# Graph attention in two layers: x projections in pieces of one row tile, with x in another buffer and the edge weights begun earlier

## The chip, the cores and the metric

The kernel runs on one core of a Trainium2 chip. The metric is the device time of one execution in microseconds, and a version of the kernel is judged by the median of its runs. All data is float32 apart from the integer adjacency matrix and a bfloat16 mask.

The core's engines appear under the names that the profile uses: PE is TensorE (its weight loads are shown apart, as PEld), DVE is VectorE, ACT is ScalarE, POOL is GpSimd, and SP is SyncE, which here issues every DMA. Each engine works through its own queue in order and waits on semaphores for the others.

## What is computed

There are 8 entries (the batch), each with 2048 nodes of 256 features. One adjacency matrix of 2048 x 2048 is shared by all. Two layers of graph attention follow one another, each with a residual and a layer norm:

```python
# layer 0: 8 heads of 32 features, prior = adj
x_proj = einsum('bnd,hdf->bhnf', x, W)
e = leaky_relu(e_src[..., :, None] + e_dst[..., None, :], 0.2)
e = e + softplus(beta_tilde) * log(prior + 1e-6)
attn = softmax(where(adj > 0, e, neg_inf), axis=-1)
x = layernorm(x + (attn @ x_proj, heads side by side) @ W_out.T)
# layer 1: one head, 256 features
h1, h2, h3 = x @ W1, x @ W2, x @ W3
attention = softmax(where(adj > 0, leaky_relu(h1 @ h2.T, 0.2), -1e12))
x = layernorm(x + relu(attention @ h3))
```

## The kernel before

**Layer 0 without a matrix of exponentials.** The exponential of a leaky ReLU of a sum is the larger of two products of a row factor and a column factor. So for each head the kernel keeps one vector over the query nodes (`c`, broadcast to all partitions) and a few numbers for each key node (`re`). For a key tile `jt` of 128 nodes (16 tiles: `NT`) and two heads (`HP`), line 311 makes `s = max(c, re) * mt` on VectorE, 128 x 2048 for each head. `mt` is the transposed tile of edge weights, `(adj + 1e-6)**beta` where there is an edge and 0 elsewhere. Then `products` (line 336) multiplies `s` with the projected features `v` into `val`, and with the key factor into `den`: 16 and 16 matmuls with 512 columns. One such unit of work, a pair of heads and a key tile, is a *step*. An entry takes 4 x 16 = 64 steps. `s` has four buffers, which is two steps' worth.

**What comes before the steps of an entry.** `Gat.project` loads x of the entry, transposes it on TensorE (`turn`, lines 235 to 243, one call for four row tiles of 128 nodes, with ScalarE copying to `xt`), multiplies with the projection weights `wp` (line 253, four matmuls for a row tile) and lets ScalarE copy the result to `v` and `both` (lines 255 and 256). When all 16 row tiles are there, a maximum over the nodes is taken (lines 260 and 261), the factors are made (`cs`, `re`), and VectorE scales all of `v` by the key factor (line 270). For entries 1 to 7 the results go to DRAM (`v_d`, `re_d`). At last `est` is a transpose of `cs` and goes to DRAM as `c_d` (lines 277 to 280). `project` is a generator: each `yield` ends a *piece*. There are six pieces for an entry: one for each group of four row tiles, one with the maximum and the scaling of `v`, one with `est`.

**Where those pieces stand.** Entry 0 is projected alone at the start. While entry 0's 64 steps run, the loop at lines 480 to 485 puts the pieces of entries 1 to 7 between them: `(B - 1) * (NB + 2)` = 42 pieces spread evenly over 64 steps. In the same loop `later_weights` prepares the weights that are needed later, in five parts, from step 16 on at every fourth step. Its three square matrices are loaded one after another into the buffer with the tag `pen` and transposed.

**Edge weights.** They are made in entry 0 during its first 16 steps and written to DRAM (`mt_d`), from where all later steps load them (`load_mt`, line 183). `make_mt(jt)` loads a column block of `adj` (tag `d`, two buffers), converts it (VectorE, line 168), takes a logarithm and an exponential (ScalarE, lines 169 and 170), masks it (VectorE, line 171), transposes the sixteen blocks on TensorE (line 176, result `mtp`), copies them to `mt` with ScalarE (line 177) and stores that. `m` has the tag `p` with two buffers; `x` of the entries being projected (`xr`, 1 MB for half an entry) has the same tag and shares these two buffers. In step `jt`, `make_mt` runs for tile `jt + 1`, before the step's own `s` and products.

**What sets the order.** TensorE's instructions run exactly in the order in which the program writes them. For the other engines, and for SyncE's DMA issues, the framework picks an order when the kernel is compiled, by priority and by when things would be ready. A buffer is handed to its next tile when the last reader of the old tile is done.

**What follows.** From entry 1 on, a step of layer 0 for the next entry is woven into layer 1 of the current one (`Dot`). `Dot.scores` uses the tag `pen` for the mask of a row tile, one buffer, and `p` for the scores.

Of the kernel before, what the change touches and what calls it, by code (L numbers as in the profile page):

```python
# [9 lines left out]
F32 = mybir.dt.float32  # L10
# [8 lines left out]
P = 128  # L19
# [8 lines left out]
def kernel(  # L28
# [26 lines left out]
    nc = tc.nc  # L55
    B, N, D = x.shape
    H, _, DH = w_proj.shape
    NT = N // P
    KC = D // P
    BK = 512  # L60
    NB = N // BK
# [3 lines left out]
    IG = BK // P  # L65
# [6 lines left out]
    wide = ctx.enter_context(tc.tile_pool(name="wide", bufs=2))  # L72
# [5 lines left out]
    def mm_tile(name):  # L78
        return ps.tile([P, BK], F32, tag="mm", name=name)

    def wide_tile(name, tag, bufs, dtype=F32):
        return wide.tile([P, N], dtype, tag=tag, name=name, bufs=bufs)
# [6 lines left out]
    ident = const.tile([P, P], F32)  # L89
# [14 lines left out]
    nc.vector.scalar_tensor_tensor(beta[:, 3:4], beta[:, 0:1], 0.0, beta[:, 2:3], ALU.max, ALU.add)  # L104
    beta_c = beta[:, 3:4]

    def load_x(b, half):
        xr = wide.tile([P, NT // 2, D], F32, tag="p", name="xr", bufs=2)
        nc.sync.dma_start(xr, x[b].rearrange("(t p) d -> p t d", p=P)[:, ts(half, NT // 2), :])
        return xr  # L110

    first_x = [load_x(0, half) for half in range(2)]


    wp = const.tile([P, KC, D + 2 * H], F32)
# [17 lines left out]
    def later_weights():  # L133

        nc.sync.dma_start(w3s, w3.rearrange("(k p) d -> p k d", p=P))
        w1t, w2t = (chunk.tile([P, KC, D], F32, tag="pt", name=name, bufs=2) for name in ("w1t", "w2t"))
        for w, dst in ((w_out, wot), (w1, w1t), (w2, w2t)):
            src = wide.tile([P, KC, D], F32, tag="pen", name="square", bufs=1)
            nc.sync.dma_start(src, w.rearrange("(k p) c -> p k c", p=P))
            yield  # L140
            for kc in range(KC):
                t = mm_tile("sq_t")
                for o in range(KC):
                    nc.tensor.transpose(t[:, ts(o, P)], src[:, o, ts(kc, P)], ident)
                nc.scalar.copy(dst[:, kc, :], t[:, 0:D])
        yield
        for dc in range(KC):
            t = mm_tile("w12p")
            for kc in range(KC):
                nc.tensor.matmul(t[:, 0:D], w1t[:, kc, ts(dc, P)], w2t[:, kc, :], start=(kc == 0), stop=(kc == KC - 1))  # L150
            nc.scalar.copy(w12[:, dc, :], t[:, 0:D])
        yield
# [7 lines left out]
    rec_d = dram.tile([B, NP, 4, HALF], F32, name="rec_d")  # L160
    x1_d = dram.tile([B, N, D], F32, name="x1_d")

    def make_mt(jt):

        a = wide.tile([P, NT, P], I32, tag="d", name="adj_t", bufs=2)
        nc.sync.dma_start(a, adj[:, ts(jt, P)].rearrange("(t p) j -> p t j", p=P))
        m = wide.tile([P, NT, P], F32, tag="p", name="m", bufs=2)
        nc.vector.tensor_scalar(m, a, 0.0, None, ALU.max)
        nc.scalar.activation(m, m, AF.Ln, bias=eps_prior)
        nc.scalar.activation(m, m, AF.Exp, scale=beta_c)  # L170
        nc.vector.scalar_tensor_tensor(m, a, 0.0, m, ALU.is_gt, ALU.mult)
        mt = wide_tile("mt", "mt", 2)
        for g in range(NB):
            t = mm_tile("mtp")
            for k in range(IG):
                nc.tensor.transpose(t[:, ts(k, P)], m[:, g * IG + k, :], ident)
            nc.scalar.copy(mt[:, ts(g, BK)], t)
        nc.sync.dma_start(mt_d[ts(jt, P), :], mt)
        return mt

    def load_mt(jt, deep):
        mt = wide_tile("mt", "d" if deep and jt % 2 else "mt", 2)
        nc.sync.dma_start(mt, mt_d[ts(jt, P), :])
        return mt
# [27 lines left out]
    def row_tile(name, bufs=4):  # L212
        return small.tile([P, D], F32, tag="row", name=name, bufs=bufs)


    class Gat:


        def __init__(self, b):
            self.b = b  # L220
            self.units = ((hp, jt) for hp in range(NP) for jt in range(NT))
            self.hts = []
            self.mts = []

        def project(self):


            b = self.b
            kept = "v" if b == 0 else ("h3", "x1t")[b % 2]
            self.v = v = whole.tile([P, NT, D], F32, tag=kept, name="v")  # L230
            both = small.tile([P, NT, 2 * H], F32, name="both", bufs=1)
            xrs, xts = [], []

            def turn(g):
                if g % 2 == 0:
                    xrs.append(load_x(b, g // 2) if b > 0 else first_x[g // 2])
                xt = chunk.tile([P, KC, BK], F32, tag="ht", name="xt", bufs=3)
                for kc in range(KC):
                    t = mm_tile("tr")
                    for k in range(IG):  # L240
                        nc.tensor.transpose(t[:, ts(k, P)], xrs[-1][:, g % 2 * IG + k, ts(kc, P)], ident)
                    nc.scalar.copy(xt[:, kc, :], t)
                xts.append(xt)

            turn(0)
            for g in range(NB):
                if g + 1 < NB:
                    turn(g + 1)
                for k in range(IG):
                    it = g * IG + k  # L250
                    t = mm_tile("proj")
                    for kc in range(KC):
                        nc.tensor.matmul(t[:, 0:D + 2 * H], xts[g][:, kc, ts(k, P)], wp[:, kc, :],
                                         start=(kc == 0), stop=(kc == KC - 1))
                    nc.scalar.copy(v[:, it, :], t[:, 0:D])
                    nc.scalar.copy(both[:, it, :], t[:, D:D + 2 * H])
                yield
            top = small.tile([P, 2, H], F32, name="top", bufs=1)
            ed, es = both[:, :, 0:H], both[:, :, H:2 * H]
            nc.vector.tensor_reduce(top[:, 0, :], ed.rearrange("p t h -> p h t"), AX.X, ALU.max)  # L260
            nc.gpsimd.partition_all_reduce(top[:, 1, :], top[:, 0, :], P, bass_isa.ReduceOp.max)
            cs = small.tile([P, H, NT], F32, name="cs", bufs=1)
            nc.vector.tensor_tensor(cs, es.rearrange("p t h -> p h t"),
                                    top[:, 1, :].unsqueeze(2).to_broadcast([P, H, NT]), ALU.add)
            nc.vector.tensor_tensor(ed, ed, top[:, 1:2, :].to_broadcast([P, NT, H]), ALU.subtract)
            self.re = re = small.tile([P, 2, NT, H], F32, name="re", bufs=2)
            nc.scalar.activation(re[:, 0], ed, AF.Exp, scale=-(1.0 - ALPHA))
            nc.scalar.activation(re[:, 1], ed, AF.Exp)
            v4 = v.rearrange("p t (h f) -> p (t h) f", f=DH)
            nc.vector.tensor_tensor(v4, v4, re[:, 1].rearrange("p t h -> p (t h)").unsqueeze(2).to_broadcast(  # L270
                [P, NT * H, DH]), ALU.mult)
            if b > 0:
                nc.sync.dma_start(v_d[b], v)
                nc.sync.dma_start(re_d[b], re)
            yield
            t = mm_tile("est")
            nc.tensor.transpose(t[:, 0:P], cs.rearrange("p h t -> p (h t)"), ident)
            est = row_tile("est")[:, 0:P]
            nc.scalar.activation(est, t[:, 0:P], AF.Exp, scale=1.0 - ALPHA)
            nc.sync.dma_start(c_d[b].rearrange("h (t p) -> (h t) p", p=P), est)  # L280
            yield
# [13 lines left out]
        def step(self, count=1):  # L295

            for _ in range(count):
                hp, jt = next(self.units)
# [3 lines left out]
                    self.den = pacc.tile([P, HALF], F32, tag="den", name="den")  # L302
                first = self.b == 0 and hp == 0
                while first and len(self.mts) < min(jt + 2, NT):
                    self.mts.append(make_mt(len(self.mts)))
                mt = self.mts[jt] if first else load_mt(jt, self.b == 0)
                s = []
                for a in range(HP):
# [4 lines left out]
                v, e = self.v, self.re[:, 1]  # L313
# [161 lines left out]
    for _ in gats[0].project():  # L475
        pass
    others = (1 for g in gats[1:] for _ in g.project())
    weights = later_weights()
    pieces = (B - 1) * (NB + 2)
    for k in range(NP * NT):  # L480
        gats[0].step()
        for _ in range((k + 1) * pieces // (NP * NT) - k * pieces // (NP * NT)):
            next(others)
        if k >= NT and k % 4 == 0:
            next(weights, None)
    for _ in others:
        pass
# [57 lines left out]
```

## Time and profile before

| | us |
|---|---|
| runs, median (lowest to highest) | 4468.5 (4466.72 to 4468.73) |
| the profiled execution | 4467.18 |
| its span in the profile | 4465.4 |
| VectorE, `s` (line 311), 1024 instructions | 2350.6 |
| TensorE, `val` (line 336), 8192 matmuls | 1045.3 |
| TensorE, `den` (line 336), 5568 matmuls | 709.2 |
| TensorE, `acc` (line 461), 4096 matmuls | 950.6 |
| last `den` of entry 0's steps ends, from the start of the span | 538.7 |

The times of instructions are busy times. Matmuls are pipelined, and the records of neighbouring ones overlap, so a busy share of TensorE near 100% means that it had work, and not that it ran at its peak. A timeline row gives a start, a time, the engine, the line, the operation with its output and inputs, how many instructions are merged in it, and in brackets how long the engine was idle just before and who released it. Rows of one engine that follow without a bracket have no gap between them. A busy share is a mean over stages with different limits, so the stretches of the span have to be looked at one by one.

### The profile page before, as it was taken

The numbers are of one execution on the slowest core, as the hardware profiler recorded it, in microseconds if no ns is written. First come the engines' busy times: TensorE is split into PE (matmuls) and PEld (weight loads), VectorE is DVE, ScalarE is ACT, GpSimd is POOL, SyncE is SP. The second block draws the span as 40 slices with busy tenths as digits, with TensorE's granted clock in tenths as the row PEclk, the third lists the DMA queues.
The fourth block names the chain that finished last, engine by engine and source line by source line (L and its number), as shares of the span: only waits on it lengthen the run. The fifth ranks groups of instructions, "written<-read, shape, count | busy, mean of one in ns | idle before, by whom it ended". The sixth has DMA issues, their size and how long they took to land.

```text
span 4465.4 us, 60558 instructions
## 1 busy us (share of the span) xinstructions
PE 4267.6 (96%) x24988; PEld 2217.3 (50%) x24988; DVE 3631.8 (81%) x2605; ACT 1758.7 (39%) x3611; POOL 7.5 (0%) x14
## 2 busy tenths in 40 slices
PE   6899899999999999999999999999999999999899
PEld 4444344445455545555455544545454554554566
DVE  5778798888989988988899888888988888898222
ACT  5622233334333343334333343333433343333555
POOL 0000000000000000000000000000000000000000
PEclk8999999999999999999999999999999999999999
DMA  7777665666555555556555565555545565553211
GB/s 217 262 264 263 249 218 204 220 233 217 180 189 193 182 193 184 188 181 224 176 182 178 186 213 187 189 181 207 194 160 190 189 216 183 187 182 134 69 50 41
DMA packets 252773, 843.62 MB, mean 189 GB/s; under 512 B 33616, under 2 KB 152400, under 8 KB 176976
## 3 DMA queue, kind: packets, MB, share of 16 engines
q1 hardware_dynamic: 252496, 839.74, 54.0%
q8 instruction: 196, 3.21, 0.3%
q14 instruction: 81, 0.66, 0.0%
HBM read 763.76 MB, written 75.37 MB: 188 GB/s over the span
## 4 chain that ended last, share of the span: by engine, by line
PE 60%; DVE 14%; issue 8%; ACT 4%; DMA 1%; SPq 0%; DVEq 0%; ACTq 0%
PE acc L461 17%; PE e L426 15%; PE val L336 12%; DVE s L311 9%; PE den L336 8%; PE pt L445 4%; DVE d L318 3%; PE h1p L416 2%; ACT p L432 1%; PE h3p L396 1%; ACT h L210 1%; DVE p L431 1%; PE y L376 1%; DMA mt<-mt_d 0%; ACT f L206 0%
## 5 line engine op out<-in xcount | busy, mean ns | idle before, releaser
L311 DVE SCALAR_TENSOR_TENSOR s<-c,re,mt 128x2048 f32<-128x2048 f32 x1024 | 2350.6, 2343 | 209.6 <-PE den L336 159.9
L336 PE MATMUL val<-s,v 128*32 128x512 f32 x8192 | 1045.3, 607 | 78.7 <-DVE s L311 78.5
L461 PE MATMUL acc<-h,pts 128*128 128x256 f32 x4096 | 950.6, 380 | 14.9 <-ACT pts L447 14.4
L426 PE MATMUL e<-x1t,h 128*128 128x512 f32 x2048 | 904.0, 594 | 0.0
L461 PEld LDWEIGHTS acc<-h,pts 128*128 128x128 f32 x4096 | 748.2, 190 | 107.7 <-ACT pts L447 21.8
L336 PE MATMUL den<-s,re 128*32 128x512 f32 x5568 | 709.2, 598 | 0.0
L318 DVE SCALAR_TENSOR_TENSOR d<-s,re,d 128x2048 f32<-128x2048 f32 x272 | 632.4, 2343 | 0.0
L426 PEld LDWEIGHTS e<-x1t,h 128*128 128x128 f32 x2048 | 379.6, 190 | 450.1 <-issue 417.9
L336 PEld LDWEIGHTS val<-s,v 128*32 128x32 f32 x8192 | 240.9, 110 | 697.8 <-issue 526.3
L447 ACT COPY pts<-pt 128x512 f32<-128x512 f32 x512 | 296.1, 583 | 664.7 <-PE pt L445 664.4
L428 ACT ACTIVATE p<-e 128x512 f32<-128x512 f32 x512 | 302.5, 595 | 432.3 <-PE e L426 432.3
L431 DVE CUSTOM_DVE_ANT_0 p<-p,pen 128x2048 f32<-128x2048 f32 x128 | 292.7, 2287 | 205.9 <-ACT p L428 205.6
L336 PEld LDWEIGHTS den<-s,re 128*32 128x32 f32 x5568 | 194.2, 112 | 426.7 <-issue 426.6
L432 ACT ACTIVATE p<-p,neg 128x2048 f32<-128x2048 f32 x128 | 256.7, 2005 | 272.5 <-DVE neg L431 272.5
L445 PEld LDWEIGHTS pt<-ident,p 128*128 128x128 f32 x2048 | 238.0, 141 | 223.5 <-issue 167.2
L445 PE MATMUL pt<-ident,p 128*128 128x128 f32 x2048 | 318.7, 279 | 5.4 <-ACT p L432 5.4
L469 DVE TENSOR_TENSOR z<-z,x1r 128x256 f32<-128x256 f32 x128 | 54.0, 422 | 205.4 <-ACT z L468 197.0
L468 ACT ACTIVATE z<-acc,rec 128x256 f32<-128x256 f32 x128 | 60.6, 473 | 355.9 <-PE acc L461 330.3
L376 PE MATMUL y<-wot,ht 128*128 128x256 f32 x512 | 129.6, 414 | 37.4 <-DVE ht L363 36.3
L206 ACT ACTIVATE f<-mv,eps_ln 128x1 f32<-128x1 f32 x256 | 74.2, 290 | 199.0 <-DVE mv L204 198.1
L396 PE MATMUL h3p<-w3s,x1t 128*128 128x256 f32 x512 | 133.4, 386 | 12.3 <-ACT x1t L392 12.3
L376 PEld LDWEIGHTS y<-wot,ht 128*128 128x128 f32 x512 | 104.7, 208 | 68.3 <-DVE ht L363 39.2
(76 smaller groups left out, 2083.6 us busy)
## 6 DMA issues: line engine op xcount, KB each, us to landing
mt<-mt_d SPq DMA_DIRECT2D x496, 1024.0 KB, 4.8
c<-c_d SPq DMA_DIRECT2D x64, 1024.0 KB, 6.7
pen<-pen_d SPq DMA_DIRECT2D x112, 512.0 KB, 3.3
xr<-in_x_dram SPq DMA_DIRECT2D x16, 1024.0 KB, 7.1
adj_t<-in_adj_dram SPq DMA_DIRECT2D x16, 1024.0 KB, 6.8
mt_d<-mt SPq DMA_DIRECT2D x16, 1024.0 KB, 5.6
rb<-rec_d SPq DMA_DIRECT2D x64, 256.0 KB, 4.0
h<-in_x_dram SPq DMA_DIRECT2D x32, 512.0 KB, 5.9
```

The costliest lines, as they stand in the source:

```text
L311: nc.vector.scalar_tensor_tensor(sa, self.cs[a], self.re[:, 0, jt, h:h + 1], mt, ALU.max, ALU.mult)
L318: nc.vector.scalar_tensor_tensor(d, sa, e[:, jt - 1, h:h + 1], d, ALU.mult, ALU.add)
L336: nc.tensor.matmul(dst[ts(q, DH), ts(c, BK)], weights[q % 2], s[q % 2][:, ds(q // 2 * HALF + c * BK, BK)], start=start, stop=stop)
L376: nc.tensor.matmul(y[:, 0:D], ht[:, ts(it, P)], wot[:, g, :], start=(g == 0), stop=(g == 1))
L396: nc.tensor.matmul(t[:, 0:D], x1t[:, kc, ts(it - 1, P)], w3s[:, kc, :], start=(kc == 0), stop=(kc == KC - 1))
L426: nc.tensor.matmul(t, self.h1[:, kc, ts(it % IG, P)], self.x1t[:, kc, ts(c, BK)], start=(kc == 0), stop=(kc == KC - 1))
L428: nc.scalar.activation(p[:, ts(c, BK)], t, AF.Prelu, alpha=ALPHA)
L431: nc.vector.tensor_tensor_reduce(p, p, pen, -1.0, FMAX, ALU.add, ALU.min, neg)
L432: nc.scalar.activation(p, p, AF.Exp, bias=neg, scale=-1.0, accum_out=den)
L445: nc.tensor.transpose(t[:, ts(k, P)], p[:, ts(g * IG + k, P)], ident)
L447: nc.scalar.copy(pt, t)
L461: nc.tensor.matmul(acc, now[:, ts(k, P)], self.h3[:, j, :], start=(j == 0), stop=(j == NT - 1))
```

## The change

Four things are edited.

1. `project` yields after each row tile instead of after each group of four, so it has `NT + 2` = 18 pieces for an entry instead of six, and the loop spreads 7 x 18 = 126 pieces over the 64 steps. The next group's `turn` is called after the first row tile of a group, where it used to be called ahead of the whole group.
2. For entries 1 to 7, `turn` loads the x of its own four row tiles (512 KB) into a tile with the tag `pen`, which has one buffer. Entry 0's x is loaded as before, into the tag `p`.
3. `make_mt` is split. `make_m` does the part up to line 171, and `make_mt` the transposes. In step `jt` of the first 16, `make_m` runs for tile `jt + 2` and then `make_mt` for tile `jt + 1`.
4. `later_weights` loads each square matrix as two row tiles (tag `row`, four buffers) with two DMAs, and its parts come at steps 18, 22, 26, 30 and 34 instead of 16, 20, 24, 28 and 32.

```diff
-    def load_x(b, half):
-        xr = wide.tile([P, NT // 2, D], F32, tag="p", name="xr", bufs=2)
-        nc.sync.dma_start(xr, x[b].rearrange("(t p) d -> p t d", p=P)[:, ts(half, NT // 2), :])
-        return xr
-
-    first_x = [load_x(0, half) for half in range(2)]
+    first_x = [wide.tile([P, NT // 2, D], F32, tag="p", name="xr", bufs=2) for _ in range(2)]
+    for half, xr in enumerate(first_x):
+        nc.sync.dma_start(xr, x[0].rearrange("(t p) d -> p t d", p=P)[:, ts(half, NT // 2), :])
...
-            src = wide.tile([P, KC, D], F32, tag="pen", name="square", bufs=1)
-            nc.sync.dma_start(src, w.rearrange("(k p) c -> p k c", p=P))
+            src = [row_tile("square") for _ in range(KC)]
+            for o in range(KC):
+                nc.sync.dma_start(src[o], w[ts(o, P), :])
...
-    def make_mt(jt):
+    def make_m(jt):
...
         nc.vector.scalar_tensor_tensor(m, a, 0.0, m, ALU.is_gt, ALU.mult)
+        return m
+
+    def make_mt(jt, m):
+
         mt = wide_tile("mt", "mt", 2)
...
             def turn(g):
-                if g % 2 == 0:
-                    xrs.append(load_x(b, g // 2) if b > 0 else first_x[g // 2])
+                if b == 0:
+                    xr = first_x[g // 2][:, ds(g % 2 * IG, IG), :]
+                else:
+                    xr = wide.tile([P, IG, D], F32, tag="pen", name="xg", bufs=1)
+                    nc.sync.dma_start(xr, x[b].rearrange("(t p) d -> p t d", p=P)[:, ts(g, IG), :])
...
             turn(0)
-            for g in range(NB):
-                if g + 1 < NB:
+            for it in range(NT):
+                g, k = divmod(it, IG)
+                t = mm_tile("proj")
+                for kc in range(KC):
+                    nc.tensor.matmul(t[:, 0:D + 2 * H], xts[g][:, kc, ts(k, P)], wp[:, kc, :],
+                                     start=(kc == 0), stop=(kc == KC - 1))
+                nc.scalar.copy(v[:, it, :], t[:, 0:D])
+                nc.scalar.copy(both[:, it, :], t[:, D:D + 2 * H])
+                if k == 0 and g + 1 < NB:
                     turn(g + 1)
-                for k in range(IG):
...
                 yield
...
                 while first and len(self.mts) < min(jt + 2, NT):
-                    self.mts.append(make_mt(len(self.mts)))
+                    at = len(self.mts)
+                    while len(self.ms) < min(at + 2, NT):
+                        self.ms.append(make_m(len(self.ms)))
+                    self.mts.append(make_mt(at, self.ms[at]))
...
-    pieces = (B - 1) * (NB + 2)
+    pieces = (B - 1) * (NT + 2)
...
-        if k >= NT and k % 4 == 0:
+        if k >= NT and k % 4 == 2:
             next(weights, None)
```

More of the change, by code (lines that the diff above doesn't have):

```diff
@@ L143, in later_weights @@
                 for o in range(KC):
-                    nc.tensor.transpose(t[:, ts(o, P)], src[:, o, ts(kc, P)], ident)
+                    nc.tensor.transpose(t[:, ts(o, P)], src[o][:, ts(kc, P)], ident)
                 nc.scalar.copy(dst[:, kc, :], t[:, 0:D])
@@ L222, in __init__ @@
             self.hts = []
-            self.mts = []
+            self.ms, self.mts = [], []
         def project(self):
@@ L231, in project @@
             both = small.tile([P, NT, 2 * H], F32, name="both", bufs=1)
-            xrs, xts = [], []
+            xts = []
             def turn(g):
-                if g % 2 == 0:
-                    xrs.append(load_x(b, g // 2) if b > 0 else first_x[g // 2])
+                if b == 0:
[3 more added lines that the diff above has]
+                    nc.sync.dma_start(xr, x[b].rearrange("(t p) d -> p t d", p=P)[:, ts(g, IG), :])
                 xt = chunk.tile([P, KC, BK], F32, tag="ht", name="xt", bufs=3)
@@ L240, in turn @@
                     for k in range(IG):
-                        nc.tensor.transpose(t[:, ts(k, P)], xrs[-1][:, g % 2 * IG + k, ts(kc, P)], ident)
+                        nc.tensor.transpose(t[:, ts(k, P)], xr[:, k, ts(kc, P)], ident)
                     nc.scalar.copy(xt[:, kc, :], t)
@@ L245, in project @@
             turn(0)
-            for g in range(NB):
-                if g + 1 < NB:
-                    turn(g + 1)
-                for k in range(IG):
[L250 to L256, printed above, removed]
+            for it in range(NT):
[7 more added lines that the diff above has]
+                if k == 0 and g + 1 < NB:
+                    turn(g + 1)
                 yield
```

## The prediction

> **What bounds the kernel now.** I read the busy shares of the page first, then its forty slices, then the busy times by stretch, then the engines' timelines over entry 0's part, and last SyncE's waits.
>
> ```profile
> PE 4267.6 (96%) x24988; PEld 2217.3 (50%) x24988; DVE 3631.8 (81%) x2605; ACT 1758.7 (39%) x3611; POOL 7.5 (0%) x14
> PE   6899899999999999999999999999999999999899
> DVE  5778798888989988988899888888988888898222
> ```
>
> A slice is 111.6 us. TensorE is below 9 in the first three slices, in the sixth and in one near the end. The change touches only what ends at about 545 us, so only there can time come or go. By stretch (span, then PE, PEld, DVE, ACT, POOL, clock, DMA share, GB/s):
>
> ```profile
> 65.30:203.80 138.50, 115.05 (x824) 68.50 (x823) 108.31 (x56) 99.48 (x156) 0.36 (x1) 0.95 0.76 245
> 410.00:470.00 60.00, 55.68 (x399) 24.68 (x391) 47.43 (x24) 15.06 (x46) 0.36 (x1) 0.97 0.72 267
> ```
>
> In the first stretch, where `m` is made, no engine is full: steps 1 to 14 go from the `val` at 67.26 to that at 203.76, 10.5 us each. VectorE waits in nearly every one, for a buffer of `m` or for `mt`:
>
> ```profile
> 188.21 2.28 DVE L171 SCALAR_TENSOR_TENSOR m<-adj_t,m 128x2048 f32<-128x2048 int32 x1
> 193.21 1.23 DVE L168 TENSOR_SCALAR m<-adj_t 128x2048 f32<-128x2048 int32 x1 [2.71 <-PE mtp L176]
> 194.35 4.61 DVE L311 SCALAR_TENSOR_TENSOR s<-c,re,mt 128x2048 f32<-128x2048 f32 x2
> 204.62 4.62 DVE L311 SCALAR_TENSOR_TENSOR s<-c,re,mt 128x2048 f32<-128x2048 f32 x2 [3.46 <-ACT mt L177]
> ```
>
> In the second stretch TensorE is the bound, with one hole per entry, where VectorE scales all of `v` (L270) while two steps follow one another with no projections between them:
>
> ```profile
> 466.44 4.43 DVE L270 TENSOR_TENSOR v<-v,re 128x4096 f32<-128x4096 f32 x1 [0.64 <-ACT re L268]
> ...
> 413.92 1.04 PE L336 MATMUL val<-s,v 128*32 128x512 f32 x2 [2.57 <-DVE s L311]
> 416.18 2.78 PE L336 MATMUL val<-s,v 128*32 128x512 f32 x11 [1.22 <-DVE s L311]
> 417.91 1.06 PE L336 MATMUL den<-s,re 128*32 128x512 f32 x1
> 418.74 1.02 PE L336 MATMUL val<-s,v 128*32 128x512 f32 x3
> 418.76 2.72 PE L336 MATMUL den<-s,re 128*32 128x512 f32 x15
> 421.42 0.33 PE L277 MATMUL est<-ident,cs 128*128 128x128 f32 x1
> ```
>
> The first is VectorE's row of the next hole, the rest TensorE's of this one; the hole returns at 473.19, 59.3 us later. The step takes 421.42 - 413.92 = 7.50 us, against 1.74 + 1.72 = 3.46 for the undisturbed one at 421.67 to 425.13. With the idle 2.57 before it that is 6.6 us lost for each entry; of the 4.0 inside the step 1.22 is idle and 2.8 is slow clock.
>
> Two rows show what a load of x will meet:
>
> ```profile
> L372 SPq DMA_DIRECT2D h<-in_x_dram x4: 384/427/497, 483.3 to 496.4; - x4
> DMA to landing us min/median/max: 6.0/6.5/8.3
> SPq L183 <- DVE s L311: 120.7, 29, 7.9
> ```
>
> The `h` load is the same shape as the new one: four row tiles of x, 512 KB. The last line is SyncE's wait between 200 and 540 us: 120.7 us in all it stood at an `mt` load waiting for `s`, 29 times, 4.2 us on average.
>
> **What the Trainium skill says.** "TensorE: Matmul & The Clock Gate", Part 1 (the HAM clock gate): after an idle window of about 3.4 us the clock falls to half, until about 3.4 us of work. The trace agrees: the step above runs at half speed after 2.57 + 1.22 us idle. "DMA: Bandwidth & Descriptors", Anatomy of one DMA: a DMA's semaphore wait is held by the issuing sequencer, not by the DMA engines; the 120.7 us agree, and what is queued behind waits too. "Trainium Kernel Development and Optimization", Best Practices, asks for double buffers to overlap DMA with compute; the new x buffer is single, which no row of before shows.
>
> **The change part by part.**
>
> *Pieces.* 42 pieces become 7 x 18 = 126, so a step gets two instead of two in three. Piece n falls in step (n+1)/2 at first, later in (n+2)/2; entries start in steps 0, 9, 18, 27, 37, 46, 55. TensorE's work is unchanged: 32 matmuls for a step 3.46 us, a row tile 3.8/4 = 0.95, a turn of 8 transposes 0.93. Each change between `den`, projections and `val` costs about 0.1 (`den` 1.83 instead of 1.72 when transposes follow; 16 projections 3.86 instead of 3.76 when `val` follows). About 22 more steps hold filler, two changes each, 4.4 us; a fifth of it lies in VectorE's shadow: +3.5.
>
> *x in the mask's single buffer.* `turn(0)` and `turn(1)` both stand in an entry's first piece. The load for `turn(1)` can't be issued until the 8 transposes of `turn(0)` release the buffer, and TensorE takes its orders as written: all later `val` and `den` wait behind these transposes, and VectorE after them, since four `s` buffers are two steps. Load 6.5 us from issue (the `h` row). SyncE stands at an `mt` load 120.7/340 = 36% of the time, for about 2.1 more us when met halfway, so with its other queueing (`v_d`, L273, and the rest) I take 1.2. Cover: the two copies of `xt` (0.59 us each, the last ends some 0.75 after the transposes) are followed by the first row tile's 0.95 and nothing else. Of the time from release only the row tile is work, and with the gap between turn and row tile counted as lost: 6.5 + 1.2 - 0.95 + 0.45 for the wake-up and issue = 7.2 idle. Slow clock after it: 2.8, as in the step above. So 10.0 per entry. Bounds: 6.0 landing with a free SyncE and one slow window, 7; 8.3 landing behind `v_d`'s 2 MB (itself 6.5 us to landing), 18. The other two turns have four pieces, two steps, about 12 us, for the same 7.7: nothing. The next entry's first load has five steps.
>
> *What that hides.* In the new order an entry's `v` scaling (piece 16) stands one step before this wait. While TensorE waits for x, VectorE does its 6 us (`top`, `cs`, `both`, 4.43) and the next two `s`. So the 6.6 us hole should go: it is replaced, not added to. Entries 2 to 7 had it after step 14: 6 x 6.6 = -40. Entries 3 to 7 get the new one there: 5 x 10.0 = +50. Net +10.
>
> *m two tiles ahead, and alone in its buffers.* L171 leaves the path from L168 to the transposes of the same step, and x no longer takes one of `m`'s two buffers. A step then needs, of VectorE, by the spacing of its rows, 2 x 2.27 + 1.15 + 2.2 = 7.9, with entry 1's `v` work spread over 13 steps 8.4; of TensorE, 1.87 for `mtp` + 3.46 + 2 x 0.95 + 0.47 for turns = 7.7, with entry 2's x wait 8.5; of ScalarE 4.0 (L169, L170) + 2.05 (L177) + 1.1 + 0.6 = 7.8. Three engines near 8.5 with a step of lead will not keep exactly to it: 9.3 taken, bounds 8.5 and 10.2. 13 steps x (9.3 - 10.5) = -15.6 (-26 to -4).
>
> *Step 0.* Entry 1's first x wait falls between the first `den` (ended at 65.3) and step 1's `mtp`, which followed at 65.33. TensorE is at half clock there already, so only the idle is added, +7; VectorE runs out, since the next `mt` lies behind it. Bounds 4 and 9.
>
> *Start.* Entry 0's `turn(1)` was hidden before the wait for `wp` (its copies end at 13.9, projections begin at 20.71); now it follows the first row tile: its 8 transposes, 1.04 us at 25.89 for such a turn: +1. `m` 0 and 1 can't start sooner than their x buffers come free; the first `s` waits for `c`, not `m`.
>
> *End.* Entry 7's `v` scaling moves from step 62 to after step 63. VectorE had 10.97 us idle there, before 546.02, which hides its 6; but `v_d` (2 MB) and `c_d` now stand on SyncE ahead of entry 1's loads: +3 (0 to 7). `est` of entries 4 to 7 follows one bare step after the last row tile, so TensorE waits about 0.5 for `cs`: +2.
>
> *Weights.* Six loads of 128 KB instead of three of 256 (3.4 us to landing), used four steps later; SyncE's 6.8 us of waits for that slot go. 28 loads of x for 14 add 14 x 0.38 us of issue. Both beside other work: 0. If SyncE's slack went, at most those 5 us spread over 500.
>
> Sum: 3.5 + 10 - 15.6 + 7 + 1 + 3 + 2 = +10.9. The profiled execution took 4467.2 us (span 4465.4 and 1.8 around it), so 4478.1; the median 4468.5 lies 1.3 higher: **4479 us**.
>
> **Rivals.** (a) *The pace decides, not slower.* If steps 1 to 13 run at 8.5 us (-26), x lands within 6.0 with SyncE free (7 us each, five of them 35 against 40: -5, and step 0 +4), and of the rest 6.5 stays (nothing at the end), the sum is -20.5: 4448. For it: no engine is over 84% in that stretch, and most of VectorE's idle there is the named wait for `m`'s buffer. Against: three engines would be near full at once. It decides once the pace is under about 8.9. (b) *They cancel.* Pace 8.8 (-22), the rest as in the sum, +4.5: 4473. (c) *x behind v_d.* SyncE stands at `v_d` until the scaling is done (it waited for `v` 24.6 us in six times), then 2 MB go ahead of x: 18 us for four of the waits instead of 10, +32 more: 4511. For it: the scaling and the release of the buffer are within a few us. Against: in entries 2 and 3 the release is 5 us earlier. That the holes of `v` stay beside the new ones would cost the 40 again; nothing but VectorE taking `v` before a ready `s` could do that, so it is in (c). That nothing changes can't be: the order on TensorE is written out.
>
> **How the numbers follow.** A measurement here tells 0.2% (8.9 us) from no change. Chances: the forecast 0.40, (a) 0.28, (b) 0.20, (c) 0.12. Slower by over 0.2%: 0.40 + 0.12 = 0.52; within: 0.20; faster: 0.28. The forecast alone with its own bounds: 4470 to 4494. To leave out no more than 2 in 10, half of (a) and most of (c) come in: 4448 to 4506.
>
> **What would show it.** In the profile after: TensorE's second turn of each entry waiting for its x load, about 7 us, seven times; the `val` waits after L270 gone; steps 1 to 14 at about 9.3 us with L168's waits gone; step 1's `mtp` near 73 us; all after the end of entry 0 as it was. The forecast is wrong if the x wait is under 4 us, if the pace is under 8.8, or if `v` and x waits stand side by side.

## The result and the profile after

| | before | after |
|---|---|---|
| median, us (runs) | 4467.61 (4) | 4470.17 (4, from 4468.95 to 4472.24) |
| ratio, 95% interval | | 1.0007 [0.9989, 1.0024] |
| profiled execution, span | 4467.18, 4465.4 | 4468.95, 4467.2 |

No change that can be told from noise. Before has four runs in this table, one more than in the one further above, so its median differs a little. The likeliest case of the prediction, 10.9 us slower, did not come. The total is that of rival (b), "they cancel", but by other terms than (b) gave, as shown below. The page after, first the shares, then TensorE's and VectorE's slices:

```profile
PE 4270.9 (96%) x24988; PEld 2216.7 (50%) x24988; DVE 3633.3 (81%) x2605; ACT 1758.5 (39%) x3611; POOL 7.5 (0%) x14
PE   6898899999999999999999999999999999999899
DVE  5877798888889988988999888888988888898222
```

The shares have not moved. To see what cancelled, one needs the same point of the work in both timelines (start of the first `val` matmul of a step, us from the span's start):

| point | before | after | after less before |
|---|---|---|---|
| first `s` on VectorE | 53.94 | 56.73 | +2.8 |
| step 1 | 67.26 | 77.80 | +10.5 |
| step 14 | 203.76 | 194.87 | -8.9 |
| step 16 | 218.33 | 206.55 | -11.8 |
| last `est`, end of entry 0's steps | 538.67 | 533.83 | -4.8 |
| first step of entry 1 | 548.93 | 549.40 | +0.5 |
| span | 4465.4 | 4467.2 | +1.8 |

So the change loses 10.5 us up to step 1, wins 19.4 in steps 1 to 14 and another 2.9 up to step 16, loses 7.0 up to the last step and 5.3 at the join to entry 1. The lines of the kernel after are new: `L179` is the transposes of `m`, `L242` the load of x, `L247` the turn, `L256` the row tile, `L275` the scaling of `v`, `L319` is `s`, `L344` is `val` and `den`.

VectorE in the stretch where `m` is made, after the change:

```profile
101.84 1.22 DVE L167 TENSOR_SCALAR m<-adj_t 128x2048 f32<-128x2048 int32 x1
102.98 4.61 DVE L319 SCALAR_TENSOR_TENSOR s<-c,re,mt 128x2048 f32<-128x2048 f32 x2
107.51 2.28 DVE L170 SCALAR_TENSOR_TENSOR m<-adj_t,m 128x2048 f32<-128x2048 int32 x1
110.03 1.23 DVE L167 TENSOR_SCALAR m<-adj_t 128x2048 f32<-128x2048 int32 x1 [0.25 <-PE mtp L179]
```

One step is 110.03 - 101.84 = 8.2 us, and of the wait for a buffer of `m`, 2.71 us in the prediction's row, 0.25 is left. Two long ones stay in the stretch, 7.63 us before 77.91 and 4.43 before 163.19, and each ends behind an x wait of TensorE. TensorE's own wait for `m` is gone there. Before, it was 18.4 us in five times, the longest 7.0:

```profile
PE mtp L176 <- DVE m L171: 18.4, 5, 7.0
```

Over steps 1 to 14, with entry 2's x wait among them, a step takes (194.87 - 77.80)/13 = 9.0 instead of 10.5.

TensorE at entry 6's first piece, where the hole of 6.6 us was before:

```profile
418.38 0.30 PE L282 MATMUL est<-ident,cs 128*128 128x128 f32 x1 [0.42 <-DVE cs L268]
418.61 1.92 PE L344 MATMUL val<-s,v 128*32 128x512 f32 x16
420.35 1.90 PE L344 MATMUL den<-s,re 128*32 128x512 f32 x16
422.18 1.09 PE L247 MATMUL tr<-ident,xg 128*128 128x128 f32 x8
423.51 1.21 PE L256 MATMUL proj<-wp,xt 128*128 128x272 f32 x4 [0.24 <-ACT xt L248]
428.25 1.94 PE L247 MATMUL tr<-ident,xg 128*128 128x128 f32 x8 [3.53 <-DMA xg<-in_x_dram]
429.98 1.84 PE L256 MATMUL proj<-wp,xt 128*128 128x272 f32 x4
431.75 1.92 PE L344 MATMUL val<-s,v 128*32 128x512 f32 x16
```

No `val` waits for `s` there. The second turn waits 3.53 us for its load, and then takes 429.98 - 428.25 = 1.73 us instead of 0.87, the row tile 1.77 instead of 1.0: the slow clock. TensorE's waits for that load in all, and the time the loads took from issue:

```profile
PE tr L247 <- DMA xg<-in_x_dram: 26.2, 7, 6.9
DMA to landing us min/median/max: 3.7/4.7/9.4
```

Seven waits, 26.2 us. With 0.24 before each row tile (1.7) and 1.4 to 2.6 us of slow clock after each (12.8 over the seven, group by group against the same group at full clock) that is 40.7, or 5.8 for an entry.

The join, SyncE and VectorE after the change. Entry 1's `re` stands behind the store of 1/`den`, which waits for the reciprocal, which waits for four small DMAs, issued after the 2 MB load of `v`:

```profile
533.37 0.38 SPq L290 DMA_DIRECT2D v<-v_d  x1
536.04 2.41 SPq L361 DMA_DIRECT2D rc<-dn  x4
541.84 0.35 DVE L362 RECIPROCAL rc<-rc 128x32 f32<-128x32 f32 x1 [4.45 <-DMA rc<-dn]
542.22 0.33 SPq L363 DMA_DIRECT2D rec_d<-rc  x1
543.91 0.89 SPq L292 DMA_DIRECT2D re<-re_d  x2
546.80 2.35 DVE L319 SCALAR_TENSOR_TENSOR s<-c,re,mt 128x2048 f32<-128x2048 f32 x1 [4.61 <-DMA re<-re_d]
```

### The profile page after: what moved, and what is told of

Its sections match the earlier page's. It is cut to its first block, busy times and chain, and to the rows that moved or that the text cites. A ratio compares the mean times of both kernels' runs of the same rounds, so it can differ in the third digit from the quotient of the medians.

```text
span 4467.2 us, 60614 instructions
## 1 busy us (share of the span) xinstructions
PE 4270.9 (96%) x24988; PEld 2216.7 (50%) x24988; DVE 3633.3 (81%) x2605; ACT 1758.5 (39%) x3611; POOL 7.5 (0%) x14
## 4 chain that ended last, share of the span: by engine, by line
PE 59%; DVE 15%; issue 8%; ACT 4%; DMA 2%; SPq 0%; DVEq 0%
PE acc L469 16%; PE e L434 15%; PE val L344 11%; DVE s L319 10%; PE den L344 8%; PE pt L453 4%; DVE d L326 3%; PE h1p L424 2%; ACT p L440 1%; PE h3p L404 1%; PE y L384 1%; DVE p L439 1%; ACT h L213 1%; DMA mt<-mt_d 0%; ACT f L209 0%
## 5 line engine op out<-in xcount | busy, mean ns | idle before, releaser
L319 DVE SCALAR_TENSOR_TENSOR s<-c,re,mt 128x2048 f32<-128x2048 f32 x1024 | 2351.8, 2343 | 213.5 <-PE den L344 167.2
L344 PE MATMUL val<-s,v 128*32 128x512 f32 x8192 | 1033.0, 605 | 62.1 <-DVE s L319 62.0
L344 PE MATMUL den<-s,re 128*32 128x512 f32 x5568 | 695.7, 595 | 0.0
L344 PEld LDWEIGHTS val<-s,v 128*32 128x32 f32 x8192 | 237.5, 110 | 666.8 <-issue 534.4
L344 PEld LDWEIGHTS den<-s,re 128*32 128x32 f32 x5568 | 190.7, 111 | 424.5 <-issue 424.5
L256 PE MATMUL proj<-wp,xt 128*128 128x272 f32 x512 | 140.7, 416 | 11.3 <-DVE wp L125 8.5
```

The lines of the kernel that those rows point to most:

```text
L319: nc.vector.scalar_tensor_tensor(sa, self.cs[a], self.re[:, 0, jt, h:h + 1], mt, ALU.max, ALU.mult)
L344: nc.tensor.matmul(dst[ts(q, DH), ts(c, BK)], weights[q % 2], s[q % 2][:, ds(q // 2 * HALF + c * BK, BK)], start=start, stop=stop)
```

## The experiments

Twelve kernels ran. Times are medians of 4 to 13 runs; the difference is to the kernel before on the same chip. An interval is some 4 to 8 us to each side, so smaller differences between two kernels are not shown.

| run | us | less before, us | ratio, 95% interval |
|---|---|---|---|
| the change | 4470.17 | +2.6 | 1.0007 [0.9989, 1.0024] |
| e1 turn after the third row tile | 4438.23 | -30.4 | 0.9929 [0.9917, 0.9942] |
| e2 m one tile ahead | 4469.77 | +1.2 | 1.0004 [0.9995, 1.0012] |
| e3 pieces of four | 4491.42 | +22.8 | 1.0052 [1.0039, 1.0065] |
| e4 v in four | 4480.85 | +12.2 | 1.0026 [1.0017, 1.0036] |
| e5 third buffer for re | 4472.09 | +3.3 | 1.0007 [0.9999, 1.0016] |
| e6 e1 and entry 0's turns as before | 4434.18 | -34.6 | 0.9924 [0.9912, 0.9937] |
| e7 e6 and third buffer | 4433.25 | -35.5 | 0.9919 [0.9906, 0.9931] |
| e8 no v scaling | 4466.12 | -2.6 | 0.9991 [0.9982, 0.9999] |
| e9 re loaded early | 4467.57 | -1.5 | 0.9997 [0.9989, 1.0005] |
| e10 e6 and re loaded early | 4430.08 | -39.0 | 0.9909 [0.9894, 0.9924] |
| e11 e1, no v scaling | 4427.27 | -41.8 | 0.9905 [0.9892, 0.9919] |
| e12 before, with fine pieces alone | 4445.60 | -23.4 | 0.9947 [0.9934, 0.9959] |

**e1: the x wait taken away**

```diff
-                if k == 0 and g + 1 < NB:
+                if k == 2 and g + 1 < NB:
                     turn(g + 1)
```

> The changed kernel with each group's next turn called after the third row tile instead of the first, so that a piece with a turn no longer holds a second one and the load of x has two pieces, about a step, to land. In the changed kernel the seven waits for x are 26.2 us of idle TensorE, and with the slow clock after them and the gap before the row tile I count 40.7 us. Theory A (the x wait covers the v scaling, it did not come on top of it): the x waits go, but at about each entry's end TensorE now waits for s behind L275, some 3 us each; the end of entry 0's steps comes 15 to 25 us earlier, the total is 4445 to 4458. Rival B (x waits and v scaling have nothing to do with one another): all of the 40 us comes back, 4430. Rival C (the join after step 63 is set by SyncE's queue whatever comes before): the steps end earlier and the join takes it back, 4467 to 4471.

4438.23 us, 33 us better than the change against their own befores: between A (4445 to 4458) and B (4430). Rival C falls, and A promised too little, since 33 of the counted 40.7 us came back. The edit also moved entry 0's turns, and the first `val` came 4.7 us later than in the change (63.85 instead of 59.14; e6 takes that up). An x wait of 1.15 us was left at entry 5. TensorE at the same place of entry 6:

```profile
394.35 1.90 PE L344 MATMUL den<-s,re 128*32 128x512 f32 x16
396.18 1.09 PE L247 MATMUL tr<-ident,xg 128*128 128x128 f32 x8
397.51 2.13 PE L256 MATMUL proj<-wp,xt 128*128 128x272 f32 x8 [0.24 <-ACT xt L248]
399.57 1.05 PE L344 MATMUL val<-s,v 128*32 128x512 f32 x2
401.34 1.49 PE L344 MATMUL val<-s,v 128*32 128x512 f32 x11 [0.73 <-DVE s L319]
```

With no x wait to cover it, the scaling of `v` leaves TensorE 0.73 us idle, at full clock. So the x wait was hardly needed to hide it. From here on there was a theory D: the pieces of one row tile hide it.

**e2: m's lead taken back, its buffers kept**

```diff
-                    while len(self.ms) < min(at + 2, NT):
+                    while len(self.ms) < min(at + 1, NT):
```

> The changed kernel with m begun one tile ahead of its transposes' step as before the change (make_m for tile jt + 1 in step jt); m still has its two buffers for itself. Theory A (the lead of a tile is what took the first 16 steps from 10.5 to 9.0 us): steps 1 to 14 at 10 us or more, the steps end 10 to 15 us later, 4478 to 4485. Rival B (it is the buffers that x no longer takes): steps 1 to 14 stay near 9.0 us, 4468 to 4472.

Rival B is right. Steps 1 to 14 took (195.0 - 78.7)/13 = 8.9 us, as with the lead. So the lead of one more tile shows no worth here. What is left of the edit is that x no longer sits in one of `m`'s two buffers; whether that is enough by itself, e3 tells.

**e3: pieces of four**

```diff
-                yield
+                if k == IG - 1:
+                    yield
...
-    pieces = (B - 1) * (NT + 2)
+    pieces = (B - 1) * (NB + 2)
```

> The changed kernel with pieces of four row tiles again (42 pieces), x still in the mask's single buffer and m two tiles ahead. Theory A: the pieces of one row tile are worth little by themselves, since TensorE's work is the same and the bound of most steps; what they do is put the v scaling next to the x wait. With pieces of four a step without projections falls between the two, so the v hole (6.6 us) comes back beside the x wait in the later entries: 4480 to 4505. Rival B (fine pieces only cost switches): 4462 to 4468, some 5 us faster than the changed kernel.

4491.42 us, as A said; rival B falls. Both holes stand in the same entry, TensorE at entry 7:

```profile
492.21 1.04 PE L345 MATMUL val<-s,v 128*32 128x512 f32 x2 [2.59 <-DVE s L320]
494.48 2.38 PE L345 MATMUL val<-s,v 128*32 128x512 f32 x11 [1.22 <-DVE s L320]
...
513.29 1.06 PE L247 MATMUL tr<-ident,xg 128*128 128x128 f32 x8 [2.66 <-DMA xg<-in_x_dram]
```

The first two rows are the hole of before (2.57 and 1.22 there). That it came back fits D as well as A, since both pieces and the distance to the x wait changed.

This run also bears on `m`. x is out of its buffers here, and TensorE has no wait for `m` there; yet steps 1 to 14 take (202.27 - 71.06)/13 = 10.1 us, not 9.0. In that stretch TensorE waits 5.5 us behind entry 1's scaling of `v`, 4.3 for x in two waits, one more than after the change, and 9.4 for ScalarE's copies of `mt` and `xt`. So the free buffers need the fine pieces to gain the 19.4 us.

**e4: the scaling of v in four**

```diff
-            nc.vector.tensor_tensor(v4, v4, re[:, 1]...)
...
-            yield
+            for i in range(n):
+                part = ts(i, NT * H // n)
+                nc.vector.tensor_tensor(v4[:, part, :], v4[:, part, :], ...)
+                ...
+                yield
...
-    pieces = (B - 1) * (NT + 2)
+    pieces = (B - 1) * (NT + 5)
```

> The changed kernel with the scaling of v for entries 1 to 7 cut into four instructions, each in a piece of its own (147 pieces), everything else as changed. Theory A (the x wait already hides the v scaling, but for entry 5, where TensorE waited 5.55 us for s): only that hole goes, total 4460 to 4470. Rival B (the scaling still costs its 6 us in every entry, and the x wait its own): 25 to 40 us faster, 4430 to 4445.

10 us slower than the change: no theory had that. VectorE and TensorE at entry 7:

```profile
479.38 4.62 DVE L281 TENSOR_TENSOR v<-v,re 128x1024 f32<-128x1024 f32 x4
...
473.07 1.92 PE L349 MATMUL val<-s,v 128*32 128x512 f32 x16
...
476.52 1.90 PE L349 MATMUL val<-s,v 128*32 128x512 f32 x16
478.24 1.90 PE L349 MATMUL den<-s,re 128*32 128x512 f32 x16
480.07 0.33 PE L287 MATMUL est<-ident,cs 128*128 128x128 f32 x1
480.33 1.04 PE L349 MATMUL val<-s,v 128*32 128x512 f32 x2
486.32 2.78 PE L349 MATMUL val<-s,v 128*32 128x512 f32 x11 [4.94 <-DVE s L324]
```

The four parts run one right after the other in 4.62 us: the compiled order did not spread them. And the added pieces hold no TensorE work, so that three steps now follow one another bare, that is with no projections between them (they start at 473.07, 476.52 and 480.33). In the third the hole is there again with 4.94 us, and the x wait comes on top of it. The same three in a row stand at entry 6, with 4.92.

How many steps are bare in a row tells the kernels apart. The kernel before has five at entry 6 (404.28, 407.74, 413.92, 421.67 and 425.13), with the hole before the third; this is where VectorE's scaling falls:

```profile
404.28 1.92 PE L336 MATMUL val<-s,v 128*32 128x512 f32 x16
...
407.74 1.90 PE L336 MATMUL val<-s,v 128*32 128x512 f32 x16
```

e3 has five as well. The change and e1 have two there (414.32 and 418.61; 388.31 and 392.61) and no such hole, and so has e12 below. These counts are read at one or two entries of a kernel; no run changes the count alone, so that it sets the hole is argued from them. A bare step takes TensorE 3.46 us and VectorE, for its two `s`, about 4.5, so that VectorE falls behind in it; a step with two row tiles takes 5.6, and there VectorE gains about 1.0. `s` has buffers for two steps, and VectorE's lump is 6 us. The change at entry 5 shows that two can be too many: VectorE had just spent 4.6 us on `ht` (2.28 waiting for `rb`, 2.29 at work), and TensorE waited 5.55:

```profile
345.47 2.29 DVE L371 TENSOR_TENSOR ht<-ht,rb 128x2048 f32<-128x2048 f32 x1 [2.28 <-DMA rb<-rec_d]
352.08 4.42 DVE L275 TENSOR_TENSOR v<-v,re 128x4096 f32<-128x4096 f32 x1
358.82 2.78 PE L344 MATMUL val<-s,v 128*32 128x512 f32 x11 [5.55 <-DVE s L319]
```

**e5, e7, e9: the join**

```diff
-    self.re = re = small.tile([P, 2, NT, H], F32, name="re", bufs=2)
+    self.re = re = small.tile([P, 2, NT, H], F32, name="re", bufs=3)
```

> The changed kernel with a third buffer for re, so that entry 1's re can be loaded before entry 7's is stored. Entry 1's first s waited 4.61 us for that load, which stood on SyncE behind the store of 1/den. Theory A (the join took back the 5 us that the steps had won, by the queue on SyncE): the load goes early, the first val of entry 1 comes 5 to 9 us sooner, total 4461 to 4466. Rival C (the join is set by the reciprocal and by ht, which wait for DMAs behind the 2 MB load of v): s comes early but the first y stays where it is, 4468 to 4471.

> The kernel of e6 with the third buffer for re as well. If e5's and e6's gains add: e6's time less 5 to 7 us, 4423 to 4429 by theory A of both; 4430 to 4440 if either fails.

Nothing came of the buffer in either: e5 is at the change's time, e7 at e6's. In e5's trace the load of `re` still stands behind the store of 1/`den` on SyncE. e9 adds a `load_re` to the third buffer, called in step 58:

```diff
     for k in range(NP * NT):
+        if k == 58:
+            gats[1].load_re()
         gats[0].step()
```

> The changed kernel with entry 1's re loaded in step 58 into a third buffer; in e5 the third buffer alone left the load where it was, behind the store of 1/den on SyncE. Theory A (the order on SyncE at the join took back what the steps had won): entry 1's first s no longer waits for re, its first val comes 5 to 9 us sooner after the last est, total 4461 to 4466. Rival C (1/den and ht bind the join): s is sooner, but the first y stays 24 us after the last est, 4468 to 4472.

TensorE in e9, where the last `est` is at 537.26:

```profile
543.77 3.43 PE L348 MATMUL val<-s,v 128*32 128x512 f32 x16 [6.20 <-DMA v<-v_d]
...
550.56 0.70 PE L388 MATMUL y<-wot,ht 128*128 128x256 f32 x2
564.60 10.13 PE L388 MATMUL y<-wot,ht 128*128 128x256 f32 x30 [13.34 <-DVE ht L375]
```

Entry 1's first `val` comes 6.5 us after the last `est` instead of 15.6, as A said, and then `y` waits 13.34 us for `ht`. Rival C holds for the place: 1/`den` and `ht` bind the join, with y's bulk 27 us after the last `est` instead of 24. The time is the change's within the interval, between what A and C had promised.

**e6: the start**

```diff
+                if b == 0 and k == 0 and g + 1 < NB:
+                    turn(g + 1)
                 t = mm_tile("proj")
...
-                if k == 2 and g + 1 < NB:
+                if b > 0 and k == 2 and g + 1 < NB:
```

> The kernel of e1_turn_late with entry 0's own turns called ahead of each group again, as before the change. Its first val stood at 63.9 us, against 56.3 before the change and 59.1 after it, since entry 0's x buffers, which m takes next, come free later. Theory A (a late m 0 and 1 delays the first step): first val near 57, total 4430 to 4434. Rival B (VectorE makes up for the start in the first 16 steps anyway): 4437 to 4440.

The diff is against e1. The first `val` stands at 55.6 us, and the median is at the edge of A's range. Against e1 it is 4 us better, which the intervals do not separate.

**e8 and e11: the scaling of v left out**

```diff
-            nc.vector.tensor_tensor(v4, v4, ...)
+            if b == 0:
+                nc.vector.tensor_tensor(v4, v4, ...)
```

> The changed kernel without the scaling of v by the key factor for entries 1 to 7 (L275 left out there; the stored v is the unscaled one). It asks what that scaling still costs in the changed kernel, the x waits being as they were. Theory A (the x wait hides it, but for entry 5): 5 to 9 us faster, 4461 to 4465. Theory D, formed on e1 (pieces of one row tile hide all but 1 to 2 us of it with no help of the x wait): the same but for entry 5 and some 7 x 1, 4456 to 4463. Rival B (it costs its 6 us in every entry): 4425 to 4435.

> The kernel of e1 (no x waits) without the scaling of v for entries 1 to 7 (left out; the stored v is the unscaled one). It asks whether the x wait was what hid the scaling. Theory A (it was, so without x waits the scaling costs some 3 us for each entry): 15 to 25 us faster than e1, 4413 to 4423. Theory D (the pieces of one row tile hide nearly all of it by themselves): 3 to 12 us faster than e1, 4426 to 4435.

With the x waits there, the scaling costs 5 us (+2.6 to -2.6), without them 11 (-30.4 to -41.8), which is 1.6 for an entry. D holds in e11, and A does not. In e8 the gain is a little under what both had promised, and its interval overlaps that of the change.

**e12: the pieces alone, on the kernel before**

```diff
                     nc.scalar.copy(both[:, it, :], t[:, D:D + 2 * H])
-                yield
+                    yield
...
-    pieces = (B - 1) * (NB + 2)
+    pieces = (B - 1) * (NT + 2)
```

> The kernel before the change with one part of it alone: pieces of one row tile, 18 for an entry; turns stay ahead of their group, x stays in m's buffers, m as before. Theory D (fine pieces take the 6.6 us hole of v out, whatever x does): entries 3 to 7 take 53 to 55 us each instead of 59, the total is 4435 to 4452. Theory A (the hole went because the x wait covered it): without x waits a hole of 3 us or more stays in each entry, 4452 to 4466. Rival E (fine pieces are worth nothing alone): 4466 to 4475.

4445.60 us: D is right. From one entry's first `est`-led step to the next (404.2, 458.1) it is 53.9 us instead of 59.3. The same place of entry 6, and a step in the stretch where `m` is made:

```profile
399.91 1.92 PE L336 MATMUL val<-s,v 128*32 128x512 f32 x16
...
403.97 0.30 PE L277 MATMUL est<-ident,cs 128*128 128x128 f32 x1 [0.42 <-DVE cs L263]
404.20 1.92 PE L336 MATMUL val<-s,v 128*32 128x512 f32 x16
405.94 1.90 PE L336 MATMUL den<-s,re 128*32 128x512 f32 x16
407.77 1.99 PE L241 MATMUL tr<-ident,xr 128*128 128x128 f32 x16
409.60 2.10 PE L253 MATMUL proj<-wp,xt 128*128 128x272 f32 x8
411.63 1.05 PE L336 MATMUL val<-s,v 128*32 128x512 f32 x2
412.94 1.49 PE L336 MATMUL val<-s,v 128*32 128x512 f32 x11 [0.26 <-DVE s L311]
...
193.46 2.00 PE L176 MATMUL mtp<-ident,m 128*128 128x128 f32 x16 [2.44 <-DVE m L171]
```

Two steps are bare, and the hole is down to 0.26 us idle with no x wait near it. The last row shows what this kernel lacks: with x in `m`'s buffers TensorE waits for `m`, 27.2 us in twelve waits, and steps 1 to 14 take (205.5 - 69.5)/13 = 10.5 us as before.

**e10: the fastest**

It is e6 with e9's early load.

> The kernel of e6 (turns after the third row tile for entries 1 to 7, entry 0's ahead of each group) with the early load of re of e9. By theory A of e9 4425 to 4430, by rival C 4433 to 4437.

4430.08 us, at the edge of A's range, 0.9% faster than before, and than the change too. Its interval overlaps that of e6, so the early load is not shown to add to it. What is shown is that the place of the turns does.

## Why the prediction was right and where it was wrong

The time lay in the range, and the forecast's size did not come: +10.9 foreseen, +1.8 in the spans, nothing that the ratio can tell from zero. That it lay in the range owes something to luck: the hole of `v`, counted at -40, went for a reason that the prediction did not have. By its steps:

| step | foreseen, us | measured, us |
|---|---|---|
| start | +1 | +2.8 (first `s`) |
| step 0, entry 1's x wait | +7 | +7.7 (step 1: +10.5, less the start) |
| m: pace of steps 1 to 14 | 9.3, so -15.6 | 9.0, so -19.4 |
| steps 14 and 15 | 0 | -2.9 |
| x wait for an entry | 10.0 | 5.8 |
| v hole | gone from six entries, -40 | gone but at entry 5, where 5.55 idle are left |
| steps 16 to 63, with x waits, v hole, pieces and `est` | +15.5 | +7.0 |
| join | +3 | +5.3 |
| after the join | 0 | +1.3 |

**Right.** The first turn and the second of an entry share a piece and a buffer, so TensorE waits once in each entry, seven times in all. Step 1's `mtp`, foreseen near 73 us, came at 75.4. The `val` waits behind the scaling of `v` went, but for the one at entry 5. The rest of the kernel stayed as it was, within 1.3 us.

**By its own signs.** It called itself wrong if the x wait was under 4 us: the waits were 26.2/7 = 3.7 us on average, six of the seven under 4. It called itself wrong if `v` and x waits stood side by side: at entry 5 they do, 5.55 and then 2.73. The pace of 9.0 was not under its 8.8. Rival (b) had the pace at 8.8 and "the rest as in the sum", and neither was so; only its total fits.

**Right by luck: step 0.** The +7 was to be idle time alone. TensorE waited 2.65 us for x there. From the end of the first `den`, at 68.47, to step 1 at 77.80 are 9.3 us instead of 1.9: besides the wait, two turns and a row tile, which stood later in the kernel before (3.2 us of work at full clock), 0.24 between them, and 1.3 of slow clock.

**Mis-sized: the x wait.** The prediction took 6.5 us for the landing and 1.2 for SyncE's queue. The loads landed in 4.7 at the median; in entry 6 the issue, at 423.30, followed the end of the transposes, at 423.27, at once. The `h` loads, of the same shape, were the nearest row, and they were slower than what they stood for. The slow clock after it was 1.8 us on average instead of 2.8. Rival (c), x behind `v_d`, was met once: in entry 2 `v_d` was issued at 148.18, x at 150.59, and TensorE waited 6.89.

**Wrong in its reason: "it is replaced, not added to".** The hole behind the scaling did go, but not because of the x wait. e12 has fine pieces and no x wait, and the hole is gone; e4 has the x wait and three bare steps, and the hole is there. The prediction saw two steps with no projections between; the timeline of before has five in a row, and VectorE's 6 us fell among them. The prediction priced the pieces at +3.5, for switches alone. By themselves they are worth -23 (e12). And the x wait, which it set off against the hole, is a cost on its own: e1 takes it away and wins 33.

**Half wrong: m.** The gain in the stretch of `m` came, a little larger. The prediction named the lead and the freed buffer together. The lead shows no worth (e2). The freed buffers took TensorE's wait for `m` away, but only together with fine pieces did that bring the 19.4 us: with free buffers and pieces of four the pace is 10.1 (e3), with fine pieces and shared buffers 10.5 (e12), with both 9.0.

**A misread line.** In the slices of before TensorE is below 9 in the first two, the fifth and the 38th, not in the first three and the sixth. Nothing in the sum hangs on it.

**The sum.** Fine pieces alone are worth -23 (e12). The rest of the change, on top of them, took 26 back. The x wait alone costs 33 (e1), so `m`, the later start and the join together leave about -7 (-23.4 in e12, -30.4 in e1), and about -11 with entry 0's turns put back (e6, -34.6). These last two are rough, as the intervals show. Not tried: the new order of the weights alone, two full buffers for x, and another order at the join that brings 1/`den` ahead of the load of `v`.

## What to carry to other kernels

When one engine has a lump of work now and then, look at what the bound engine has between its steps at that moment: filler in small pieces lets the other engine catch up, and pieces that hold no work for the bound engine make bare steps. Count the bare steps in a row: here two were mostly harmless, three and five were not. A single buffer that is filled on demand makes an engine wait for most of the load if two uses stand next to one another in that engine's fixed order (2.6 to 6.9 us each time here); moving the second use two pieces later won 0.7%, and cost 4.7 us at the start until entry 0 was left out of it (e6). When two tiles of different life share a buffer set, separate them before adding lead.

## What the runs showed of the hardware

Gaps shorter than 3.4 us can be followed by a slow clock. The Trainium skill, "TensorE: Matmul & The Clock Gate", Part 1, speaks of an idle window of about 3.4 us. After gaps of 2.63 to 2.73 us here, the eight transposes took 1.40 to 1.74 us instead of 0.87; after 0.73 us (e1) the 11 `val` matmuls took 1.49 us as at full speed. In the prediction's own example, too, neither gap, 2.57 nor 1.22, is as long as that window. Nor does the length of a gap decide alone: behind the first 32 `y` matmuls and the two `val` that follow them the gap is 2.52 us in several kernels, and the next 11 `val` took 1.49 us in the changed kernel (at 568.86) and in e6 (535.30), but 2.78 in e1 (540.01). The same page calls the window free-running, which fits, but no run here shows that it is the cause.

A load of the same shape can differ by more than twice: 512 KB of x landed between 3.7 and 9.4 us after its issue in one execution of the changed kernel.
